# Layer 2's attention: squares and norms of the first head group, times of turnings and outputs, and two longer pauses

## The chip, the cores and the metric

The kernel runs on one core of one Trainium2 chip. The metric is the device time of that core in microseconds. Three runs of the kernel before gave 3033.62, 3033.73 and 3040.51; their median is 3033.73. The profile is of one further execution, with its own time.

## The reference

The input x has the shape (2, 1024, 128) in float32, so there are 2048 tokens of 128 features. The program is a stack of four layers. Each of them adds to x half of a feed-forward block, then an attention (or another mixer of tokens), then half of the same feed-forward block again. The change touches the attention of layer 2, and the norms that open this attention and the second feed-forward block of that layer. Cut to what is computed there:

```python
x = x + 0.5 * _L2_ffn_ref(_layernorm(x), ...)      # 8 experts, 2 per token
x = x + _L2_attn_ref(_layernorm(x), norm_w, Wq, Wkv, Wo, q_gamma, k_gamma)
x = x + 0.5 * _L2_ffn_ref(_layernorm(x), ...)

def _L2_attn_ref(tokens, norm_w, Wq, Wkv, Wo, q_gamma, k_gamma):
    x = tokens * rsqrt(mean(tokens**2, -1) + eps) * norm_w
    q = x @ Wq;  k, v = split(x @ Wkv)              # 16 heads of 64
    q = q / max(norm(q), 1e-12) * (q_gamma + 1) * 8  # norm of each head
    k = k / max(norm(k), 1e-12) * (k_gamma + 1) * 8
    sim = tanh(q @ k.T / 50) * 50 * 64**-0.5         # no mask
    return (softmax(sim) @ v) @ Wo

def _L2_ffn_ref(x, ...):      # per token: the two best of 8 experts
    h = gelu(x @ w1[e] + b1[e]);  res = x + h @ w2[e] + b2[e]
    y = sum over e of gate_e * (layernorm(res) * gamma[e] + beta[e])
```

## The kernel before

**Tokens.** There are two sequences (b = 0, 1) of 1024 tokens, 16 tiles of 128 tokens in all, eight tiles for each sequence. Four tiles form a chunk; the chunks are q = 0 to 3, of which 0 and 1 belong to b = 0. The residual x stays in SBUF all the time.

**Who orders what.** The order of the instructions on TensorE (PE) is written out by hand: the region is under a manual schedule for that engine. The orders of VectorE (DVE), ScalarE (ACT), GpSimd (POOL) and of the DMA issues on SyncE (SP) are chosen by the framework's planner. Each engine then carries out its own instructions in that order and waits wherever an operand or a buffer is not ready.

**Threads.** Work beside the main loop is given as a list of pieces, each a function that issues instructions or a number, which is a pause in planned microseconds. `later` enters such a list as a thread. `tick(us)` moves the planned time forward and lets the first threads in the list issue the pieces whose time has come. `need(key)` issues all that is left of a thread at once.

**Norms.** `norm_pieces` (L183) gives the pieces of one chunk's norm: the statistics (`norm_stats`, with `inv_sqrt` at its end and the offset `ln_off` at L152), a pause `wait[0]`, the application, which writes xn (L162 and L164, L162 on VectorE and L164 on ScalarE), a pause `wait[1]`, four transposes into a PSUM bank pt (L172) and the copy xT. `wait` is (4.5, 4.0) by default, and everywhere in the kernel before. `l2_attn_prep` (L1567) uses it for the attention of one chunk q, `l2_ffn_prep` (L1241) for one of the two chunks (a = 0, 1) of a half of layer 2's feed-forward block; the half's name begins with 1 in the first such block of the layer and with 2 in the second. The second block takes the chunks 0 and 2 as one half and 1 and 3 as the other. `inv_sqrt` (L107) computes a reciprocal square root by Newton's method, in two plus nine small VectorE instructions.

**One group of heads.** `L2Attention.project(b, f)` (L1580) sets up four heads (f = 0 to 3) of one sequence. It returns eight products and eight turnings, one for each tile j. `product(j)` multiplies the normed tokens with the weights for v (pv, L1597) and for q and k (pqk, L1601), copies v (L1598) and q and k (raw, L1608) to SBUF with VectorE, squares raw (sq, L1610) on GpSimd, and sums the squares by head with VectorE into hsq (L1611). The last of the eight also issues the max with 1e-24 (L1614) and `inv_sqrt`, which gives hrq for all eight tiles. `turn(j)` multiplies raw by hrq (L1619, VectorE), transposes q and k with TensorE (four transposes into a bank ppt, L1623) and writes the result, times gamma, to tr (L1626, VectorE).

**The first group.** Its pieces (`first(a)`, a = 0, 1) run as threads inside the last experts of layer 2's first feed-forward block, before the attention's own loop begins. first(0) holds the products 0 to 3; first(1) holds the products 4 to 7 and then all eight turnings.

**The loop.** `run` (L1648) goes through the eight groups, which I count as n = 0 to 7 (b first, then f), each in 16 steps. A step takes two of the group's four heads (p), one half of the queries and two tiles of keys. It issues

- the scores ps (L1687) with a tanh (L1694) on ScalarE for each of two tiles of keys, and one exp (L1695) over both;
- the mix of the step before (po, L1720, TensorE) with the sums of the exponentials: acp on GpSimd (L1707 to L1710), acc on VectorE (L1712 to L1716);
- in every fourth step the division of a finished block: its sums by head in a bank pn (L1732), a copy to rn on ScalarE (L1734), its reciprocal (L1735) and the product aoT (L1736), both on VectorE;
- the pieces that belong to this step: in the steps 0 to 7 one product of the next group each; its eight turnings in the steps 10, 11, 12, 12, 13, 13, 14, 14; and the four pieces of the output of the group before (py, L1664, TensorE) in the steps 8, 8, 9, 9. The second and the fourth of these add a full bank py to four tiles of x (L1673, VectorE);
- `tick(5.8)`.

The last group (n = 7) has no next group; in its step 10 it issues the first two pieces of its own output too. When a group with f = 3 has added its part to x, `done` enters the norms of the second feed-forward block for those chunks. So there are norms in n = 1 (chunks 2 and 3, for the attention of sequence 1) and in n = 4 (the chunks 0 and 1, which group 3's output has finished, for the second feed-forward block).

**PSUM.** There are two buffers for the pairs ps, two for the sums po, and two banks that pt, pv, pqk, ppt, py and pn share in turn.

**Experts and transfers.** An expert step of layer 2 has products ph (L1454), gelu (L1463, ScalarE), products py (L1470) and a result res (L1488), which is stored by SyncE (yd, L1502). `l2_back` (L1524) brings the results back to the tokens with 16 gathers on GpSimd's queue (yg, L1539), which wait for the last such store, and adds them to x with VectorE (L1556).

Of the kernel before, what the change touches and what calls it, by code (L numbers as in the profile page):

```python
# [11 lines left out]
F32 = mybir.dt.float32  # L12
I32 = mybir.dt.int32
BF16 = mybir.dt.bfloat16
AF = mybir.ActivationFunctionType
ALU = mybir.AluOpType
# [5 lines left out]
TB = 8  # L22
# [81 lines left out]
        nc.scalar.copy(out, in_)  # L104


def inv_sqrt(c, out, in_, scale, eps):  # L107


    v = c.nc.vector  # L110
    shape = list(in_.shape)
    flat = int(np.prod(shape[1:]))
    t = c.act.tile(shape, F32, tag=f"nw{flat}", name="nw", bufs=2)
    h = c.act.tile(shape, F32, tag=f"nh{flat}", name="nh", bufs=2)
    v.tensor_scalar(h, in_, scale, eps, ALU.mult, ALU.add)
    v.tensor_scalar(out.bitcast(I32), h.bitcast(I32), -0.5, float(0x5F3759DF), ALU.mult, ALU.add)
    for _ in range(3):
        v.tensor_mul(t, out, out)
        v.scalar_tensor_tensor(t, h, -0.5, t, ALU.mult, ALU.mult)
        v.scalar_tensor_tensor(out, t, 1.5, out, ALU.add, ALU.mult)  # L120
# [1120 lines left out]
def l2_ffn_prep(c, w, keep, h, a):  # L1241
    nc = c.nc
    q, r = h["qs"][a], {}
    tiles = slice(4 * a, 4 * a + 4)
    norm = norm_pieces(c, r, q, by=8)

    def begin():
        if "o" not in h:
            h["o"] = keep.tile([P, 2, TB, 8], F32, tag="ho", name="ho", bufs=2)
            h["g"] = keep.tile([P, 2, TB], F32, tag="hg", name="hg", bufs=2)  # L1250

    def store():
        nc.sync.dma_start(out=h["xd"][512 * a : 512 * a + 512, :].rearrange("(j p) d -> p j d", p=P), in_=r["xn"])

    def chosen():
        h["ready"] += 1
        if h["ready"] == 2:
            c.later(("route", h["name"]), l2_route(c, w, keep, h) + h["then"])

    gates = gate_pieces(  # L1260
        c, r, q, w["router"], 8, w["beta"],
        places=lambda: ([h["o"][:, k, tiles, :] for k in range(2)], [h["g"][:, k, tiles] for k in range(2)]),
    )
    return [begin] + norm[:3] + [store] + norm[3:] + gates[:1] + [chosen] + gates[1:]
# [302 lines left out]
def l2_attn_prep(c, w, rs, q):  # L1567

    e = float(np.finfo(np.float32).eps)
    return norm_pieces(c, rs[q], q, 1.0 + e, 1e-5 * e, w["norm"])  # L1570


class L2Attention:
# [6 lines left out]
    def project(self, b, f):  # L1580


        c, nc, w, rs = self.c, self.c.nc, self.w, self.rs
        side, bank = self.side, c.bank
        mine = self.pool if f % 2 else side
        raw = side.tile([P, TB, 2, 4, 64], F32, tag="raw", name="raw")
        tr = mine.tile([P, 2, 2, S], F32, tag="tr", name="tr", bufs=1)
        v = mine.tile([P, TB, 4, 64], F32, tag="v", name="v", bufs=1)
        ssq = side.tile([P, TB, 2, 4], F32, tag="hsq", name="hsq", bufs=2)
        rq = side.tile([P, TB, 2, 4], F32, tag="hrq", name="hrq", bufs=2)  # L1590

        def product(j):
            c.need((self.key, 2 * b + j // 4))
            lhsT = rs[2 * b + j // 4]["xT"][:, j % 4 * P : (j % 4 + 1) * P]
            pv = bank("pv")[:, 0:256]
            off = 1024 + f * 256
            nc.tensor.matmul(pv, lhsT=lhsT, rhs=w["wkv"][:, off : off + 256], start=True, stop=True)  # L1597
            nc.vector.tensor_copy(v[:, j].rearrange("p h d -> p (h d)"), pv)  # L1598
            pp = bank("pqk").rearrange("p (n h d) -> p n h d", n=2, h=4)
            for n, wt in enumerate((w["wq"], w["wkv"])):  # L1600
                nc.tensor.matmul(  # L1601
                    pp[:, n].rearrange("p h d -> p (h d)"),
                    lhsT=lhsT,
                    rhs=wt[:, f * 256 : (f + 1) * 256],
                    start=True,
                    stop=True,
                )
            nc.vector.tensor_copy(raw[:, j], pp)  # L1608
            sq = side.tile([P, 2, 4, 64], F32, tag="sq", name="sq", bufs=1)
            nc.gpsimd.tensor_mul(sq, raw[:, j], raw[:, j])  # L1610
            nc.vector.tensor_reduce(ssq[:, j], sq, AX.X, ALU.add)  # L1611
            if j == TB - 1:

                nc.vector.tensor_scalar(ssq, ssq, 1e-24, None, ALU.max)  # L1614
                inv_sqrt(c, rq, ssq, 1.0, 0.0)

        def turn(j):
            rj = raw[:, j]
# [16 lines left out]
    def first(self, a):  # L1635

        if a == 0:
            self.ready, self.products, self.turns = self.project(0, 0)
        pieces = []
        for p in self.products[4 * a : 4 * a + 4]:  # L1640
            pieces += [p, 1.0]
        if a == 1:
            pieces.append(3.0)
            for p in self.turns:
                pieces += [p, 1.0]
        return pieces

    def run(self, done, room, even):  # L1648

        c, nc, w = self.c, self.c.nc, self.w  # L1650
        with c.pool("l2a", 2) as pool:
# [94 lines left out]
            for n, (b, f) in enumerate(groups):  # L1746
                (tr, v), aoT = ready, [pool.tile([P, S], F32, tag="aoT", name="aoT", bufs=3) for _ in range(2)]
                slots = [[] for _ in range(16)]
                if n + 1 < len(groups):
                    ready, first, second = self.project(*groups[n + 1])  # L1750
                    for s, piece in enumerate(first):
                        slots[s].append(piece)
                    for s, piece in zip((10, 11, 12, 12, 13, 13, 14, 14), second):
                        slots[s].append(piece)
                for s, piece in zip((8, 8, 9, 9), outs):
                    slots[s].append(piece)
                for s in range(16):
                    k2, often = s % 4, n + 1 == len(groups) and s >= 10
# [504 lines left out]
```

## Time and profile before

| Profiled execution | |
|---|---|
| its own time | 3029.26 us |
| span of its instructions | 3027.5 us |
| mean granted TensorE clock | 0.94 |
| PE busy | 2630.6 us (87%) |
| DVE busy | 2062.3 us (68%) |
| ACT busy | 1596.4 us (53%) |
| POOL busy | 1012.2 us (33%) |
| tanh of layer 2's attention (L1694), 256 of them | 249.0 us, mean 1021 ns |
| exp (L1695), 128 of them | 244.6 us, mean 1911 ns |
| squares (L1610), 64 of them | 88.7 us on POOL, mean 1386 ns |

How to read it: times are microseconds from the start of the span unless they are called ns. A row of the trace gives the start of an instruction, or of several of a kind in a run (x8), the time from its start to its end, the engine, the source line, and what is written and read by the program's names. Brackets at its end hold the time for which the engine stood idle before it, and what it waited for. The granted clock is the share of TensorE's full clock that the chip gave in that stretch. Busy shares are means over stages with different limits; what bounds one stage is read from that stage.

### The profile page before, as it was taken

To read this page: it belongs to the slowest core of one execution; us is meant where nothing else is said; L and a number is where in the kernel's file an instruction comes from. 1 tells how busy PE (TensorE), PEld (TensorE's weight loads), DVE (VectorE), ACT (ScalarE), POOL (GpSimd) and SP (SyncE) were. 2 spreads that over 40 slices of the span, in tenths; PEclk is the share of its full clock that TensorE was granted. 3 is DMA by queue.
4 is the path that set the end of the run, shared out by engine and by line. 5 is a ranking of instruction groups with operands and counts; after the bars stand their busy time and mean duration, and the time that the engine had idled before them with its cause. 6 is when DMAs were issued, how large, how long until landed. Compare 5 with 4: busy or idle time off the path is not lost. (4 is left out here: it accounts for less than half of the span.)

```text
span 3027.5 us, 42431 instructions
## 1 busy us (share of the span) xinstructions
PE 2630.6 (87%) x14226; PEld 1508.3 (50%) x14226; DVE 2062.3 (68%) x6460; ACT 1596.4 (53%) x3188; POOL 1012.2 (33%) x941
## 2 busy tenths in 40 slices
PE   8899999899998888988867569899989996859999
PEld 5544444444574644444447543333434433756667
DVE  5566667666648887688574368867787765557884
ACT  3455555455442465666423327577767784434553
POOL 0133332233104554454333444344434433322110
PEclk9899999999999788999988889899999998979999
DMA  4000000000000000000105510000000012630000
GB/s 122 14 9 14 15 15 15 7 15 15 22 1 0 1 1 1 1 1 1 57 17 153 153 43 1 1 1 1 1 8 1 1 62 74 170 94 21 1 5 11
DMA packets 69768, 86.52 MB, mean 29 GB/s; under 512 B 14334, under 2 KB 49935, under 8 KB 68912
## 3 DMA queue, kind: packets, MB, share of 16 engines
q1 hardware_dynamic: 60816, 71.71, 8.4%
q0 software_dynamic: 4992, 10.27, 1.7%
q8 instruction: 114, 1.87, 0.3%
q10 hardware_dynamic: 3744, 1.84, 0.2%
q14 instruction: 102, 0.84, 0.1%
HBM read 66.18 MB, written 12.38 MB: 26 GB/s over the span
## 5 line engine op out<-in xcount | busy, mean ns | idle before, releaser
L1694 ACT ACTIVATE pe<-ps 128x1024 f32<-128x1024 f32 x256 | 249.0, 1021 | 208.1 <-PE ps L1687 203.3
L518 ACT ACTIVATE pe<-ps,nm 128x512 f32<-128x512 f32 (+3 forms) x384 | 219.8, 578 | 144.9 <-DVE nm L516 121.8
L1687 PE MATMUL ps<-tr 64*128 64x512 f32 x1024 | 263.5, 634 | 0.0
L1720 PE MATMUL po<-pe,v 128*64 128x512 f32 x1024 | 250.1, 609 | 1.4 <-ACT pe L1695 1.4
L1695 ACT ACTIVATE pe<-pe 128x2048 f32<-128x2048 f32 x128 | 244.6, 1911 | 4.0
L348 DVE SCALAR_TENSOR_TENSOR x<-py,gates,x 128x128 f32<-128x128 f32 x448 | 133.3, 344 | 138.7 <-PE py L311 122.7
L516 DVE TENSOR_REDUCE nm<-ps 128x2 f32<-128x256 f32 (+1 forms) x192 | 183.2, 954 | 59.6 <-PE ps L505 55.6
L1454 PE MATMUL ph<-xgT,w1b 128*128 128x128 f32 x736 | 117.4, 311 | 94.0 <-ACT hT L1463 81.4
L505 PE MATMUL ps<-kT,qT 64*128 64x512 f32 (+3 forms) x768 | 180.2, 547 | 16.4 <-ACT pe L518 9.2
L1463 ACT ACTIVATE hT<-ph,w1b 128x128 f32<-128x128 f32 x368 | 105.1, 369 | 160.0 <-issue 112.6
L533 PE MATMUL ptp<-ident,pe 128*128 128x128 f32 x1152 | 172.6, 284 | 16.0 <-ACT pT L104 9.4
L533 PEld LDWEIGHTS ptp<-ident,pe 128*128 128x128 f32 x1152 | 123.8, 141 | 116.6 <-issue 56.2
L547 PE MATMUL po<-pT,v 128*64 128x512 f32 (+3 forms) x768 | 166.7, 513 | 0.0
L1454 PEld LDWEIGHTS ph<-xgT,w1b 128*128 128x128 f32 x736 | 104.4, 219 | 103.5 <-ACT hT L1463 87.0
L1707 POOL TENSOR_TENSOR acp<-pe 128x1024 f32<-128x1024 f32 x32 | 78.3, 2446 | 220.0 <-ACT pe L1695 197.0
L1720 PEld LDWEIGHTS po<-pe,v 128*64 128x64 f32 x1024 | 62.7, 137 | 174.8 <-issue 159.9
L104 ACT COPY pT<-ptp 128x512 f32<-128x512 f32 x192 | 91.9, 478 | 108.2 <-PE ptp L533 107.5
L1396 POOL DMA_INDIRECT xg<-xd,r_tok x92 | 87.6, 952 | 168.2 <-DVE res L1488 96.3
L1687 PEld LDWEIGHTS ps<-tr 64*128 64x128 f32 x1024 | 90.8, 191 | 104.5 <-issue 73.8
L1072 POOL TENSOR_SCALAR pe<-pe,rs 128x256 f32<-128x256 f32 (+7 forms) x128 | 95.2, 757 | 139.4 <-DVE rs L1069 56.0
L311 PEld LDWEIGHTS py<-l3f_w,hT 128*128 128x128 f32 x1024 | 125.6, 195 | 28.1 <-issue 23.3
L1610 POOL TENSOR_TENSOR sq<-raw 128x512 f32<-128x512 f32 x64 | 88.7, 1386 | 147.4 <-DVE raw L1608 113.2
(418 smaller groups left out, 6279.4 us busy)
## 6 DMA issues: line engine op xcount, KB each, us to landing
w1b<-sets SPq DMA_DIRECT2D x92, 258.0 KB
b2g<-sets SPq DMA_DIRECT2D x92, 128.0 KB
two<-two SPq DMA_DIRECT2D x64, 128.0 KB
yd<-y SPq DMA_DIRECT2D x20, 258.0 KB
l2f_w<-in_l2f_w SPq DMA_DIRECT2D x2, 2048.0 KB
sets<-in_l2f_w SPq DMA_DIRECT2D x1, 2048.0 KB
xd<-xn SPq DMA_DIRECT2D x8, 256.0 KB
l3f_w<-in_l3f_w SPq DMA_DIRECT2D x2, 1024.0 KB
```

The source lines that it names most:

```text
L311: nc.tensor.matmul(py[:, j, :], lhsT=hT[:, k, j * P : (j + 1) * P], rhs=w2[:, e, k, :], start=(k == 0), stop=(k == hc - 1),)
L348: c.nc.vector.scalar_tensor_tensor(x, py[:, j, :], rs[q]["g"][:, j, e : e + 1], x, ALU.mult, ALU.add)
L505: nc.tensor.matmul(ps[:, h, :W], lhsT=u["qT"][r, q0 : q0 + P], rhs=u["kT"][r, gk * 512 : gk * 512 + W], start=True, stop=True,)
L516: nc.vector.tensor_reduce(nm, ps[:, :, :W], AX.X, ALU.max, negate=True)
L518: nc.scalar.activation(u["pe", n][:, h, i, :W], ps[:, h, :W], AF.Exp, bias=nm[:, h : h + 1], accum_out=u["rs"][:, n, i, h : h + 1],)
L533: nc.tensor.transpose(pt[:, i * P : (i + 1) * P], u["pe", n][:, h, i, j * P : (j + 1) * P], c.ident)
L547: nc.tensor.matmul(u["po", n][r, lo * P :], lhsT=u["v"][:, BLOCKS[n][1] * 4 + j, cols], rhs=u["pT", n, j][h][:, lo * P :], start=(j == 0), ...
L1454: nc.tensor.matmul(ph[:, a * P : (a + 1) * P], lhsT=t[:, a * P : (a + 1) * P], rhs=xT[n][:, j * P : (j + 1) * P], start=True, stop=True,)
L1687: nc.tensor.matmul(ps[:, h, :], lhsT=tr[r, 1, p, k * P : (k + 1) * P], rhs=tr[r, 0, p, q * 512 : (q + 1) * 512], start=True, stop=True,)
L1694: nc.scalar.activation(pe[:, j], ps, AF.Tanh, scale=1.0 / 50.0)
L1695: nc.scalar.activation(pe, pe, AF.Exp, scale=50.0 * 0.125)
L1720: nc.tensor.matmul(u["po"][r, :], lhsT=u["v"][:, k, 2 * u["p"] + h, :], rhs=pe[:, j, h, :], start=(k == 0), stop=(k == TB - 1),)
```

## The change

It has four parts.

1. *The first group's squares and norms.* For b = f = 0 the squares are computed on ScalarE by an activation with Square in place of GpSimd's product. The max and `inv_sqrt` are issued after the product 3 for the tiles 0 to 3, and after the product 7 for the tiles 4 to 7. `inv_sqrt` gets a `shape`, so that its small tiles for a half keep the size that the whole has. Each half of the products is followed by its own four turnings, so first(0) now holds four products and four turnings, and first(1) the same.
2. *Turnings.* In every group the eight turnings of the next go into the steps 11, 11, 12, 12, 13, 13, 14, 14.
3. *Outputs.* The four pieces go into the steps 8, 8, 10, 10.
4. *Pauses.* `wait` is (9.0, 14.0) in the attention's norms of the chunks 2 and 3, and in the norm of the first chunk (a = 0) of each half of layer 2's second feed-forward block, that is for the chunks 0 and 1.

```diff
-def inv_sqrt(c, out, in_, scale, eps):
+def inv_sqrt(c, out, in_, scale, eps, shape=None):
...
-    shape = list(in_.shape)
+    shape = list(shape or in_.shape)
...
-    t = c.act.tile(shape, F32, tag=f"nw{flat}", name="nw", bufs=2)
-    h = c.act.tile(shape, F32, tag=f"nh{flat}", name="nh", bufs=2)
+    t = c.act.tile(shape, F32, tag=f"nw{flat}", name="nw", bufs=2)[:, 0 : in_.shape[1]]
+    h = c.act.tile(shape, F32, tag=f"nh{flat}", name="nh", bufs=2)[:, 0 : in_.shape[1]]
...
@@ l2_ffn_prep
-    norm = norm_pieces(c, r, q, by=8)
+    norm = norm_pieces(c, r, q, by=8, wait=(9.0, 14.0) if h["name"][0] == "2" and a == 0 else (4.5, 4.0))
...
@@ l2_attn_prep
-    return norm_pieces(c, rs[q], q, 1.0 + e, 1e-5 * e, w["norm"])
+    wait = (4.5, 4.0) if q < 2 else (9.0, 14.0)
+    return norm_pieces(c, rs[q], q, 1.0 + e, 1e-5 * e, w["norm"], wait=wait)
...
@@ L2Attention.project, product(j)
-            nc.gpsimd.tensor_mul(sq, raw[:, j], raw[:, j])
+            if b + f:
+                nc.gpsimd.tensor_mul(sq, raw[:, j], raw[:, j])
+            else:
+                nc.scalar.activation(sq, raw[:, j], AF.Square)
             nc.vector.tensor_reduce(ssq[:, j], sq, AX.X, ALU.add)
-            if j == TB - 1:
-                nc.vector.tensor_scalar(ssq, ssq, 1e-24, None, ALU.max)
-                inv_sqrt(c, rq, ssq, 1.0, 0.0)
+            if j == TB - 1 or b + f == 0 and j == 3:
+                js = slice(0 if b + f else j - 3, j + 1)
+                nc.vector.tensor_scalar(ssq[:, js], ssq[:, js], 1e-24, None, ALU.max)
+                inv_sqrt(c, rq[:, js], ssq[:, js], 1.0, 0.0, ssq.shape)
...
@@ L2Attention.first
-        if a == 1:
-            pieces.append(3.0)
-            for p in self.turns:
-                pieces += [p, 1.0]
+        pieces.append(3.0)
+        for p in self.turns[4 * a : 4 * a + 4]:
+            pieces += [p, 1.0]
...
@@ L2Attention.run
-                    for s, piece in zip((10, 11, 12, 12, 13, 13, 14, 14), second):
+                    for s, piece in zip((11, 11, 12, 12, 13, 13, 14, 14), second):
...
-                for s, piece in zip((8, 8, 9, 9), outs):
+                for s, piece in zip((8, 8, 10, 10), outs):
```

## The prediction

> **What bounds the kernel now.** I began with the page's slices (each digit is the busy tenths of 1/40 of the span, 75.7 us). Layer 2's attention fills slices 25 to 34 of 40, about 1802 to 2545 us:
>
> ```profile
> PE   8899999899998888988867569899989996859999
> ...
> PEclk9899999999999788999988889899999998979999
> ```
>
> TensorE (PE) is at nine tenths in most of them. The page's own chain of waits covers only the last tenth of the span (its shares add up to 10%), so it says nothing here; I went to busy time by stretch (columns: us, then busy time of PE, weight loads, VectorE, ScalarE, GpSimd, then the granted clock):
>
> ```profile
> 1890.00:1980.00 90.00, 78.19 (x326) 32.67 (x324) 70.48 (x160) 55.46 (x49) 31.07 (x17) 0.91 0.00 1
> 1980.00:2070.00 90.00, 87.02 (x394) 35.91 (x392) 67.75 (x79) 64.61 (x54) 42.18 (x21) 1.00 0.00 1
> 2160.00:2250.00 90.00, 80.00 (x362) 34.58 (x360) 70.07 (x125) 58.59 (x54) 37.86 (x19) 0.96 0.01 4
> ```
>
> An undisturbed group of heads (the middle row) is bound by TensorE and has 3 us of 90 to give; the first output products of two such groups start at 2043.11 and 2131.12, so a group takes 88.0. The others lose 10 to 12 us: there a norm or an expert's result lands among the group. I call the groups n = 0 to 7; n = 2, 3, 5 and 6 are undisturbed, n = 1 and 4 are not. Then I read TensorE and VectorE in order of time. Steps 9 to 11 of n = 2 on TensorE (the brackets hold the idle time before the row and what ended it):
>
> ```profile
> 2050.81 2.05 PE L1664 MATMUL py<-l2a_wo,aoT 128*128 128x128 f32 x16 [1.01 <-DVE x L1673]
> ...
> 2056.58 0.66 PE L1623 MATMUL ppt<-ident,raw 128*128 128x128 f32 x4
> ...
> 2062.23 0.66 PE L1623 MATMUL ppt<-ident,raw 128*128 128x128 f32 x4 [1.21 <-DVE x L1673]
> ```
>
> and VectorE in the same steps:
>
> ```profile
> 2050.67 7.69 DVE L1619 TENSOR_TENSOR raw<-raw,hrq 128x512 f32<-128x512 f32 x6
> 2058.29 3.34 DVE L1735 RECIPROCAL rn<-rn 128x512 f32<-128x512 f32 x1
> 2061.55 0.62 DVE L1673 TENSOR_TENSOR x<-x,py 128x512 f32<-128x512 f32 x1
> 2062.09 0.67 DVE L1736 TENSOR_TENSOR aoT<-po,rn 128x512 f32<-128x512 f32 x1
> ...
> 2063.29 1.21 DVE L1712 TENSOR_TENSOR acc<-pe 128x1024 f32<-128x1024 f32 x1
> ```
>
> What to see: both waits of TensorE are for a PSUM bank (there are two) that VectorE's addition of py to x (L1673) has to empty, and the second addition stands directly behind the reciprocal, with aoT and acc behind it. At the start of the attention, TensorE waits, and one square on GpSimd stands in what it waits for:
>
> ```profile
> 1782.21 0.59 PE L1601 MATMUL pqk<-l2a_wkv,xT 128*128 128x256 f32 x2
> 1793.86 1.97 PE L1623 MATMUL ppt<-ident,raw 128*128 128x128 f32 x8 [11.06 <-DVE raw L1619]
> ...
> 1802.62 1.99 PE L1687 MATMUL ps<-tr 64*128 64x512 f32 x8
> ```
>
> ```profile
> 1788.09 1.05 POOL L1610 TENSOR_TENSOR sq<-raw 128x512 f32<-128x512 f32 x1
> ```
>
> That square's input was ready at 1785.74 (the copy L1608 of 1785.06 takes 0.68), but two gathers stood before it on GpSimd. From the last projection to the first scores it takes 20.4 us. Last, the norms in n = 1 and n = 4:
>
> ```profile
> 1956.49 1.11 PE L172 MATMUL pt<-ident,xn 128*128 128x128 f32 x4 [5.12 <-ACT xn L164]
> 2241.58 1.25 PE L172 MATMUL pt<-ident,xn 128*128 128x128 f32 x4 [8.16 <-ACT xn L164]
> ```
>
> ```profile
> 2241.03 1.26 ACT L164 ACTIVATE xn<-x,ln_off,ln_rs 128x128 f32<-128x128 f32 x3 [8.94 <-DVE ln_off L152]
> ```
>
> ScalarE takes its instructions in order: while it waits for ln_off, the tanh and exp behind it wait too, and TensorE behind those.
>
> **The change part by part.** I follow the order in which the changed program is built, engine by engine.
>
> *First group, first half in the experts (a loss).* Its rsqrt and its four turnings now stand before the last experts' products. The reduction of the fourth product ended at 1763.84; then come the max and 11 small instructions of 32 elements. Rows of that width in the trace (L210, L211) take 0.19 and follow each other at 0.225: 12 x 0.225 = 2.7. With one scaling (0.68) the first transpose can start at 1767.2, and the expert's ph behind it on TensorE stood at 1764.75: 2.5 late. Four groups of transposes at 0.57 add 2.3, and a clock drop after this 3.4 us gap about 1.2. Sum: 6.0. The last yd store, the 16 gathers that wait for it and products 4 to 7 move by as much.
>
> *First group, second half (a gain).* After: last projection 0.59, raw copy 0.68, square on ScalarE 0.63 (the square L828 takes 0.685 at 576 elements), reduction 0.69, 12 small ones 2.7, four scalings 2.54, then tr, transpose, tr, transpose on two banks, 1.9: 9.7 instead of 20.4, a gain of 10.7. Products 4 to 7 took 10.1 us and lose the GpSimd waits in between (1.3). So 6.0 - 10.7 - 1.3 = -6.0. GpSimd's 16 gathers at 1.255 then end near 1807 (1803.4 before), and the first square of group 1 is queued behind them; the reduction that waits for it holds VectorE's copies of the next products. With the scores 6 us earlier this costs about 0.5. **I take -5.5, with -9 and 0 as ends.**
>
> [...] The row: the page's profile has loads of 1283 ns (L300, L1911). [...] No row of before shows a square beside a gelu; but the changed program holds as many table loads as before (24), in the same order, so I take no load.
>
> *Turnings from step 11, output at 8 and 10 (a loss).* The wait of 1.01 goes, because py's second half comes a step later. But ppt at step 11 is now two turnings, and the second needs the bank that the second addition to x empties. In the changed program VectorE's order is: six scalings, reciprocal, aoT, acc<-pe, x, acc+acp. For n = 2: TensorE does the same work in steps 8 to 11 without either wait and stands before that turning at 2062.23 - 1.01 - 1.21 = 2060.0. VectorE's scalings do not come earlier (they hang on the norm of the group's heads, before step 9), so the reciprocal ends at 2061.55, aoT 0.60 later, acc 1.15 later, x 0.68 later: 2064.0. **The turning starts 1.8 us later than before, after an idle stretch of 4.0 us.** Nothing later takes it back: before, no wait over 0.3 follows in the group.
>
> Idle stretches cost clock. The rows (last stretch, PEclk third from the end):
>
> ```profile
> 2056.00:2064.00 8.00, 6.79 (x34) 1.00 0.00 0
> 1872.40:1876.00 3.60, 3.55 (x12) 0.55 0.01 2
> ```
>
> The gap of 1.21 left the clock full; that of 2.41 (before 1872.45) gave 0.55 for 3.6 us, and 2.59 (before 2264.26) 0.64 for 4.0. A gap of 4.0 then costs 3.6 x 0.45 = 1.6. [...] I take the row. **+13.6; ends -8.9 (both waits simply go, 4 x 2.22) and +16.**
>
> *n = 0 (nothing).* It has no output. The wait of 2.40 before its first turning goes, but the turnings at step 12 wait for tr behind the same VectorE chain: its reciprocal ends at 1867.9, then aoT, acc, acc+acp, tr: 1871.8, and TensorE is there at 1867. Step 12 ends near 1873 as before. 0, ends -2.4 and +1.8.
>
> *Longer pauses, n = 1.* The two transposes pt go three steps later. xn keeps its place on ScalarE, so ScalarE still waits for ln_off (7.0 and 5.3 us). TensorE gains 1.19 + 1.12 at the first, and at the second goes on with one step of scores until it meets the held tanh; the stall at step 11 takes some back. Between 0 and -8; I take -3.
>
> *Longer pauses, n = 4.* Here xn moves behind exp. Waits of 8.16, 0.88, 2.59 and 0.35 (12.0) stand against a wait of 6.4 at step 11 (the same chain with the norm's small instructions in it: x ends near 2242.8, TensorE is there at 2236.4) and gate work now among the next group's products. Between 0 and -12; I take -5.
>
> *End.* py's second half meets the last group's own output: +0.5, within 1 either way.
>
> Sum: -5.5 + 13.6 + 0 - 3 - 5 + 0.5 = +0.6. Against the profiled execution (3029.26, of which the span is 3027.5) that is 3029.9; the runs' median is 3033.73, the sum on it **3034**.
>
> **The rivals.**
> 1. *Slower.* The step-11 stall also decides n = 1 and n = 4, and the pauses give nothing: 6 x 3.4 - 5.5 + 0.5 = +15.4, 3049. For it: VectorE is busiest there (70 of 90). Against: the waits for xn are larger than the stall. It decides once x lands in these groups later than ScalarE's wait for ln_off ended before.
> 2. *Faster: the moved steps do what they say.* The four groups lose 2.22 each: 3034 - 13.6 - 8.9 = 3012. For it: nothing waits at py any more. Against: VectorE's built order.
> 3. *Faster: the pauses remove all of TensorE's waits for xn:* 6.3 and 12.0 instead of 3 and 5, 3034 - 10.3 = 3024. Against: ScalarE still stands before ln_off.
> 4. *The start gives nothing,* GpSimd's gathers being the head of the first steps: 3034 + 5.5 = 3039.5.
>
> **How the numbers follow.** A measurement of this kernel tells about 0.3% (9 us) from no change. Likeliest case 0.42 (its own range 3027 to 3041), rival 4 0.13: both within 0.3%, 0.55. Rivals 2 (0.13) and 3 (0.12): faster 0.25. Rival 1: slower 0.20. The range reaches down between rivals 2 and 3 to 3016 and up to rival 1's 3049; outside lie most of rival 2 and the upper half of rival 1.
>
> **What would show it.** First scores near 1797 with the last gather near 1807; squares of about 0.63 on ScalarE with no table load beside them; at step 11 of n = 2, 3, 5, 6 a wait of about 4 us for x with the clock near 0.5 after it, and groups 91.4 apart instead of 88.0; ScalarE still idle before xn in n = 1. I am wrong if groups come out at 86 (rival 2), or if first scores come at 1802 or later.

## The result: 3045.91 us, 0.4% slower

The changed kernel takes 3045.91 us (median of five runs, 3044.02 to 3052.21). The kernel before takes 3035.61 in the same comparison (3033.62 to 3040.51). The ratio is 1.0039 with a 95% interval of 1.0027 to 1.0051: a loss of 10.3 us in the medians, small and real. The prediction's likeliest case was 3034, with a range of 3016 to 3049; the time lies inside the range, but on the side to which I gave 0.2.

The profiled execution of the changed kernel took 3044.02 with a span of 3042.1. Read first, as before, was the busy time by stretch (columns as in the prediction). The first row is the stretch of 90 us that was undisturbed before; the others go in pieces of 4 us through step 11 of group n = 2:

```profile
1980.00:2070.00 90.00, 85.31 (x374) 35.23 (x374) 66.65 (x77) 61.43 (x51) 39.38 (x20) 0.96 0.00 1
2054.00:2058.00 4.00, 0.28 (x3) 0.05 (x1) 3.97 (x4) 0.97 (x1) 0.00 (x0) 0.92 0.00 0
2058.00:2062.00 4.00, 3.50 (x10) 1.91 (x12) 3.97 (x6) 0.27 (x1) 0.00 (x0) 0.50 0.00 0
2062.00:2066.00 4.00, 4.00 (x16) 1.02 (x13) 1.17 (x1) 3.35 (x3) 0.00 (x0) 0.73 0.00 0
```

TensorE was busy for 87.02 of that stretch and is now busy for 85.31; its clock fell from 1.00 to 0.96. In the second row it does next to nothing (0.28 of 4.00), and in the two rows after that it works at a clock of 0.50 and 0.73. TensorE in order of time shows the same place (n = 2, steps 10 to 12; lines are seven to eight higher in this kernel, so L1671 is py, L1631 ppt and L1694 ps):

```profile
2047.86 2.05 PE L1671 MATMUL py<-l2a_wo,aoT 128*128 128x128 f32 x16
...
2053.63 0.66 PE L1631 MATMUL ppt<-ident,raw 128*128 128x128 f32 x4
2058.50 1.12 PE L1631 MATMUL ppt<-ident,raw 128*128 128x128 f32 x4 [4.22 <-DVE x L1680]
2059.55 3.79 PE L1694 MATMUL ps<-tr 64*128 64x512 f32 x8
```

The wait of 1.01 at py is gone. In place of it and of the 1.21 in step 11, the second turning of step 11 waits 4.22 for the addition to x, and the scores behind it take 3.79 where they take 1.99 at full clock. VectorE in the same steps:

```profile
2045.02 7.71 DVE L1627 TENSOR_TENSOR raw<-raw,hrq 128x512 f32<-128x512 f32 x6
2052.65 3.34 DVE L1742 RECIPROCAL rn<-rn 128x512 f32<-128x512 f32 x1
2056.03 0.69 DVE L1743 TENSOR_TENSOR aoT<-po,rn 128x512 f32<-128x512 f32 x1
2056.63 1.22 DVE L1719 TENSOR_TENSOR acc<-pe 128x1024 f32<-128x1024 f32 x1
2057.77 0.68 DVE L1680 TENSOR_TENSOR x<-x,py 128x512 f32<-128x512 f32 x1
```

This is the order that the prediction read from the built program: scalings, reciprocal, aoT, acc, and only then x (L1680), which empties the bank. The start of the attention, on TensorE and ScalarE:

```profile
1766.34 0.63 PE L1631 MATMUL ppt<-ident,raw 128*128 128x128 f32 x4 [3.29 <-DVE raw L1627]
...
1792.16 1.97 PE L1631 MATMUL ppt<-ident,raw 128*128 128x128 f32 x8 [5.97 <-DVE raw L1627]
...
1796.51 2.67 PE L1694 MATMUL ps<-tr 64*128 64x512 f32 x8
```

```profile
1787.13 0.63 ACT L1617 ACTIVATE sq<-raw 128x512 f32<-128x512 f32 x1 [1.41 <-DVE raw L1611]
```

The first scores start at 1796.51 in place of 1802.62, and a square takes 0.63 on ScalarE.

Last, the norms in n = 1 and n = 4 on ScalarE:

```profile
1953.35 0.88 ACT L165 ACTIVATE xn<-x,ln_off,ln_rs 128x128 f32<-128x128 f32 x2 [8.42 <-DVE ln_off L153]
```

```profile
2243.85 1.26 ACT L165 ACTIVATE xn<-x,ln_off,ln_rs 128x128 f32<-128x128 f32 x3 [9.71 <-DVE ln_off L153]
```

ScalarE stands before xn no shorter than it did (8.42 here and 5.29 before for the second norm of n = 1, 9.71 and 8.94 for the first of n = 4); TensorE waits for xn at the transposes pt in neither group any more; where it waits now is told under "The pauses".

Where the time went is read from the starts of the scores. I counted from the first product of the first group (so that what lies ahead of the attention drops out), and measured each group from its step 4 to the next group's step 4, which makes one period of a group whole:

| Stretch | before | after | difference |
|---|---|---|---|
| first product to first scores | 58.50 | 51.68 | -6.8 |
| first scores to step 4 of n = 0 | 20.7 | 23.0 | +2.3 |
| n = 0 | 88.51 | 89.26 | +0.8 |
| n = 1 | 104.98 | 102.37 | -2.6 |
| n = 2 | 88.01 | 92.63 | +4.6 |
| n = 3 | 88.17 | 92.38 | +4.2 |
| n = 4 | 108.11 | 106.99 | -1.1 |
| n = 5 | 88.00 | 91.59 | +3.6 |
| n = 6 | 81.53 | 85.10 | +3.6 |
| step 4 of n = 7 to the last scores | 57.7 | 59.3 | +1.6 |
| first product to last scores | 784.29 | 794.35 | +10.1 |

The attention alone accounts for +10.1, as much as the medians differ. The two profiled executions differ by 14.8 (3044.02 and 3029.26); the rest lies outside the attention, where the program is the same. There, runs of one kernel differ by several microseconds too: the profiled execution of before was 4.4 faster than the fastest of the five runs in this comparison.

### The profile page after: what moved, and what is told of

Same layout as the page of the kernel before. It is cut to its first block, busy times and chain, and to the rows that moved or that the text cites. A ratio compares the mean times of both kernels' runs of the same rounds, so it can differ in the third digit from the quotient of the medians.

```text
span 3042.1 us, 42448 instructions
## 1 busy us (share of the span) xinstructions
PE 2630.8 (86%) x14226; PEld 1511.2 (50%) x14226; DVE 2061.9 (68%) x6472; ACT 1601.2 (53%) x3196; POOL 1001.5 (33%) x933
## 5 line engine op out<-in xcount | busy, mean ns | idle before, releaser
L1694 PE MATMUL ps<-tr 64*128 64x512 f32 x1024 | 270.9, 649 | 0.8 <-issue 0.5
L517 DVE TENSOR_REDUCE nm<-ps 128x2 f32<-128x256 f32 (+1 forms) x192 | 183.2, 954 | 59.3 <-PE ps L506 55.3
L1465 ACT ACTIVATE hT<-ph,w1b 128x128 f32<-128x128 f32 x368 | 105.0, 369 | 149.8 <-issue 95.5
L1694 PEld LDWEIGHTS ps<-tr 64*128 64x128 f32 x1024 | 92.9, 196 | 114.1 <-issue 79.3
L312 PE MATMUL py<-l3f_w,hT 128*128 128x128 f32 x1024 | 129.3, 280 | 7.3 <-issue 4.9
```

The lines of the kernel that those rows point to most:

```text
L312: nc.tensor.matmul(py[:, j, :], lhsT=hT[:, k, j * P : (j + 1) * P], rhs=w2[:, e, k, :], start=(k == 0), stop=(k == hc - 1),)
L517: nc.vector.tensor_reduce(nm, ps[:, :, :W], AX.X, ALU.max, negate=True)
L1694: nc.tensor.matmul(ps[:, h, :], lhsT=tr[r, 1, p, k * P : (k + 1) * P], rhs=tr[r, 0, p, q * 512 : (q + 1) * 512], start=True, stop=True,)
```

## The experiments

All verdicts are against the kernel before on the same chip. Kernels that are set against the same time of the kernel before shared a chip. On one chip, where the kernel before took 2944.21, the experts' stages ran faster, so its times are only compared with each other. The groups of the attention took the same time on all chips: with turnings, outputs and VectorE's work as before, groups 2 and 5 are 88.0 everywhere. Where a number is given for a group, it is from step 4 to step 4 as in the table, in one profiled execution of that kernel.

### Which of the two moves costs the time

Turnings alone:

```diff
-  zip((10, 11, 12, 12, 13, 13, 14, 14), second)
+  zip((11, 11, 12, 12, 13, 13, 14, 14), second)
```

> The kernel before with only the turnings moved (steps 11, 11, 12, ...). Theory (the loss is the pair of moves: with both, VectorE's second addition of py to x stands behind reciprocal, aoT and acc, and the second turning of step 11 waits for it): alone, this move leaves that addition directly behind the reciprocal; the waits of about 1.0 at py and 1.2 at the second turning stay, and groups 2, 3, 5 and 6 keep 88.0 us each; whole kernel within 4 us of before. Rival (each move costs by itself, half of the 16 us that the four groups lost): groups of about 90 us, whole kernel +8. Rival (the move of turnings is the loss): groups of 92, +16.

Measured: 3037.94 against 3033.17, ratio 1.0015 (1.0005 to 1.0025). Groups 2, 3, 5 and 6 take 88.01, 88.16, 88.01 and 81.53: not one of them moved by more than 0.01 against before. The waits stayed too, on TensorE of group 2:

```profile
2058.23 2.05 PE L1664 MATMUL py<-l2a_wo,aoT 128*128 128x128 f32 x16 [1.00 <-DVE x L1673]
...
2069.65 0.66 PE L1623 MATMUL ppt<-ident,raw 128*128 128x128 f32 x4 [1.21 <-DVE x L1673]
```

Moving the turnings costs and gains nothing by itself in these groups. The whole kernel is 4.8 slower, a little more than the 4 that the theory allowed. The attention took 787.5 from the first product, 3.2 more than before, of which 2.4 lie ahead of step 4 of group 0, where the edit changes nothing; I come back to that. What the rest of the 4.8 is, no run here shows.

Outputs alone:

```diff
-  zip((8, 8, 9, 9), outs)
+  zip((8, 8, 10, 10), outs)
```

> The kernel before with only the output pieces moved (steps 8, 8, 10, 10). Theory: the wait at py goes, the first turning stays in step 10, and the second, in step 11, needs the bank of the first, whose copy tr now stands behind reciprocal and aoT on VectorE: a wait of about 2.8 in place of 1.0 + 1.2, with a clock drop of about 1.4 behind it: groups of 88.0 + 0.6 + 1.4 = 90, four of them +8. Rival (this move alone is the whole loss): groups of 92, +16. Rival (the move only removes the wait): groups of 87, -4.

Measured: 3043.49 against 3033.17, ratio 1.0031 (1.0019 to 1.0044). The groups take 90.45, 91.81, 90.45 and 82.33, that is +2.4, +3.6, +2.4 and +0.8. In group 2 the turning waits 3.27 for the copy tr, and the clock falls behind it:

```profile
2069.11 0.66 PE L1623 MATMUL ppt<-ident,raw 128*128 128x128 f32 x4 [3.27 <-DVE tr L1626]
2069.69 3.39 PE L1687 MATMUL ps<-tr 64*128 64x512 f32 x8
```

So this move alone is a loss, by another operation (tr, L1626) that stands behind the same reciprocal. The four lose 9.3 in all where the theory had 8 and the rivals 16 and -4. These four also show what the clock is worth. The wait is 3.3 to 3.4 in all of them, but in n = 6 the clock stayed at 1.00 behind it, and that group lost only 0.8; behind the others it fell (0.63, 0.50 and 0.57 in the 4 us from the turning on in n = 2, 3 and 5), and they lost 2.4 to 3.6.

Both moves, with nothing else changed:

> The kernel before with both moves, and neither the change to the first group nor the pauses. Theory: the four groups take 88.0 + 4.0 = 92 as in the changed kernel, with a gap of about 4.2 in step 11 and a clock near 0.5 after it; groups 1 and 4 lose up to 3 each, the last about 1.6: +17 to +24 against before. Rival (the stall comes from the new start or the pauses, which shift the work on VectorE): 88 a group, within 4 us of before.

Measured: 3050.5 against 3033.17, ratio 1.006 (1.0043 to 1.0077), 17.3 slower. The groups take 92.90, 92.61, 92.11 and 85.66: +4.9, +4.4, +4.1 and +4.1, 17.6 in all. The stall needs neither the new start nor the pauses. Groups 1 and 4 lost nothing (104.41 and 106.31, against 104.98 and 108.11); there the theory was wrong.

The two moves taken back, start and pauses kept:

> The changed kernel with turnings and outputs put back (steps 10, 11, 12, ... and 8, 8, 9, 9). Theory: first scores 6 to 7 us earlier, 2 to 3 of it given back in the first four steps of group 0; group 1 gains 3 to 6 from the pauses; group 4 gains 10 and gives some 9 back in the first steps of group 5; four groups at 88.0. Sum -4.5 - 4 - 1.5 = -10 against before, faster by about 0.3%. Rival (the loss sits in the start or in the pauses): not faster than before.

Measured: 3026.88 against 3033.17, ratio 0.998 (0.9967 to 0.9993), 6 faster. The four groups are back at 88.01, 88.01, 88.01 and 81.52. The loss of the change is these two moves together; the rest of it is a gain. It is smaller than the 10 that were expected: the attention came 4.5 faster, since group 0 gave back 4.4 of the earlier start and not 2 to 3, and group 4 gained nothing (108.75).

### What stands in the way in step 11

First the reciprocal is taken out of the chain:

```diff
-  nc.vector.reciprocal(rn, rn)
+  nc.vector.tensor_scalar(rn, rn, 0.0, 1.0 / 1024, ALU.mult, ALU.add)
```

> The changed kernel with the reciprocal of the softmax sums (3.34 us on VectorE) replaced by a cheap operation that writes the constant 1/1024. This leaves out the division by the sums, so what follows the attention sees other values and only the groups of the attention are read. Theory (the second turning of step 11 waits for the chain reciprocal, aoT, acc, x on VectorE): the gap of 4.2 in groups 2, 3, 5 and 6 shrinks by about 2.9 to 1.3, TensorE's clock stays full after it, and these groups take 92.3 - 2.9 - 2.6 = 86.8 from step 4 to step 4. Rival (the gap belongs to something else, such as the bank's own turn or ScalarE): groups of 92 and a gap of 4 as before.

VectorE and TensorE of this kernel, group 2:

```profile
2011.35 0.41 DVE L1742 TENSOR_SCALAR rn<-rn 128x512 f32<-128x512 f32 x1
2011.80 0.69 DVE L1743 TENSOR_TENSOR aoT<-po,rn 128x512 f32<-128x512 f32 x1
2012.40 1.22 DVE L1719 TENSOR_TENSOR acc<-pe 128x1024 f32<-128x1024 f32 x1
2013.54 0.68 DVE L1680 TENSOR_TENSOR x<-x,py 128x512 f32<-128x512 f32 x1
```

```profile
2014.27 0.66 PE L1631 MATMUL ppt<-ident,raw 128*128 128x128 f32 x4 [1.29 <-DVE x L1680]
```

This is one execution of a kernel that leaves the division out, read for its groups alone. The operation takes 0.41 in place of 3.34, and the wait shrinks by the same 2.93, from 4.22 to 1.29. Behind a gap of 1.29 the clock stays at 1.00. Groups 2, 3 and 5 take 87.0, where 86.8 was expected. The wait is for VectorE's chain, and for no bank's own turn.

The second cause was the length of the scalings ahead of the reciprocal: 7.71 for six, where the first two took 1.29 (0.645 each). Here GpSimd's additions acp are left out in the block of steps 8 to 11, and with them VectorE's addition of acp to acc (1.22):

```diff
+  late = u["p"] == 1 and u["q"] == 0
-  if k2 == 0:
+  if k2 < 2 and late:
+      pass
+  elif k2 == 0:
...
-  nc.vector.tensor_add(acc, acc, acp)
+  if not late:
+      nc.vector.tensor_add(acc, acc, acp)
```

> The changed kernel without GpSimd's three additions acp in the block of steps 8 to 11, which leaves out the first half of that block's softmax sums; only the groups are read. Theory (VectorE's chain is late because its two-operand instructions hold while GpSimd adds: six scalings took 7.7 and not 6 x 0.645 = 3.9, one Newton step 2.25 and not 0.23): the scalings fall to 0.65 each, the reciprocal of step 9 begins about 5.9 earlier, the gap of 4.2 in step 11 and the clock drop vanish, groups 2, 3, 5 and 6 take about 85.5. Rival (the scalings are long for another reason): scalings of 1.28, groups of 92.

```profile
2031.33 0.22 DVE L120 SCALAR_TENSOR_TENSOR nw<-nh,nw 128x64 f32<-128x64 f32 x1
...
2035.21 3.69 DVE L1627 TENSOR_TENSOR raw<-raw,hrq 128x512 f32<-128x512 f32 x6
```

In this one execution six scalings take 3.69 and the Newton step 0.22. In the changed kernel that step took 2.25, beside the first of GpSimd's additions:

```profile
2038.87 2.40 POOL L1714 TENSOR_TENSOR acp<-pe 128x1024 f32<-128x1024 f32 x1 [1.47 <-ACT pe L1702]
```

```profile
2039.10 2.25 DVE L120 SCALAR_TENSOR_TENSOR nw<-nh,nw 128x64 f32<-128x64 f32 x1
```

Without the additions the groups take 85.51, 85.51, 85.51 and 79.03, as expected, and in group 2 TensorE waits nowhere in steps 8 to 12. These are the times of a group without any stall, and they allow a second sum: 92.63 - 85.51 = 7.1, of which 4.22 is the wait and 2.9 the clock (0.65 over the 8.00 us behind the wait, which is 2.8).

Like the Newton step, the scalings are held beside an addition. In the changed kernel GpSimd's other two additions

```profile
2044.63 2.36 POOL L1716 TENSOR_TENSOR acp<-acp,pe 128x1024 f32<-128x1024 f32 x1 [3.36 <-ACT pe L1702]
2047.07 2.70 POOL L1717 TENSOR_TENSOR acp<-acp,pe 128x1024 f32<-128x1024 f32 x1
```

run from 2044.63 to 2049.77, over the first two of the six scalings. These take 2.53 and 2.86, where the median of the eight is 0.68, and each ends some 0.55 after the addition beside it. Not every operation of VectorE is held: the reciprocal at 1979.90 in the changed kernel took 3.34 with two such additions beside it, as it does without them, and the copy tr at 1983.16, beside the second of them, took 0.63. What decides between the two kinds, no run here shows.

### The start

Norm and turnings of the first group in halves, but with the squares left on GpSimd; turnings, outputs and pauses as before:

```diff
-  nc.scalar.activation(sq, raw[:, j], AF.Square)
+  nc.gpsimd.tensor_mul(sq, raw[:, j], raw[:, j])
```

> The kernel before with the first group's norms and turnings in halves, but its squares left on GpSimd (turnings, outputs and pauses as before). From the same expert product to the first scores the kernel before takes 72.3 us, the changed one 65.5. Theory (most of the gain is the norm in halves, the squares on ScalarE only save waits behind the gathers): 67.5 to 69.5. Rival (the squares are the gain): 72 or more. Rival (they give nothing): 65.5.

This expectation was set from an expert's product, which on this faster chip stands elsewhere (the same measure gave 82.2 here and 75.5 for the run with ScalarE's squares that shared the chip, so that the squares are worth 6.7 by it). I therefore read it from the first product of the first group to the first scores. Without any change that stretch took 58.5, 58.6, 58.9 and 58.8 (four kernels); with squares on ScalarE it took 51.4 to 52.1 in nine; with halves and squares on GpSimd it took 60.1. One execution took 2948.41, where the kernel before has 2944.21 on that chip. The theory was wrong and the rival that puts the gain in the squares right: against the run that shared the chip (51.4), the squares are worth 8.7, more than the whole gain of 7, and the halves without them lose about 1.4 (there is no trace of the kernel before on that chip; the 58.5 to 58.9 are from the other). From the last projection's end to the first scores it takes 19.8 before, 15.5 with halves alone, and 10.3 with both. The halves do gain at the end, but they spend it earlier, in the experts, where their rsqrt and turnings come ahead of the last products; the squares on ScalarE gain in the projections and behind the gathers.

What the start gained is partly given back in the first steps of group 0: from first scores to step 4 it takes 20.7 to 23.0 in the four kernels with the old start, and 22.0 to 26.1 in the nine with the new one. Not all of that belongs to the start. In the kernel with only the turnings moved, the first mix of group 0 waits 2.07 and then runs for 3.22, where before it waited 1.42 and ran for 1.94, with the same program in both. From the scores ahead of that mix to the pqk behind it takes 8.11 there and 5.81 before, so that such a wait and the slower products behind it account for some 2 us from one kernel's trace to another's.

### The pauses

The feed-forward norm's pauses put back, start and the attention's pauses kept:

> Start and the longer pauses of the attention's norms alone: the changed kernel with turnings, outputs and the feed-forward norm's pauses put back. Theory (the feed-forward pauses only move 10 us of waits from group 4 to the first steps of group 5): from step 4 of group 4 to step 4 of group 5 it takes 108.1 as in the kernel before, against 108.75 with these pauses; whole kernel within 3 us of the run with both pauses, 8 faster than before. Rival (these pauses are worth the forecast 5 once the stall is gone): 5 slower than with both.

Measured: 2934.48 against 2944.21, ratio 0.9966 (0.9952 to 0.9981), 9.7 faster. Group 4 takes 106.44 without these pauses and 108.75 with them. In other kernels that leave its norms and its outputs alone it takes 108.1 to 110.3, so that a gain of 2.3 from taking them away is not settled, but the forecast gain of 5 from having them is not there. Why they give nothing is to be seen in the run with both pauses (TensorE and ScalarE, group 4):

```profile
2236.06 3.68 PE L1727 MATMUL po<-pe,v 128*64 128x512 f32 x8 [8.03 <-ACT pe L1702]
```

```profile
2233.72 0.49 ACT L165 ACTIVATE xn<-x,ln_off,ln_rs 128x128 f32<-128x128 f32 x1 [8.93 <-DVE ln_off L153]
```

The wait of 8.16 at the transposes pt is gone, and TensorE waits 8.03 at the mix po: ScalarE still stands 8.93 before xn until ln_off is there, with the exp that po needs queued behind it. The pauses moved TensorE's place of waiting, not ScalarE's. Two pairs of kernels that differ in the pauses of both norms, and in the start, say the same of the time: group 4 takes 108.75 with them and 108.11 without where turnings and outputs are as before, and 106.99 with and 106.31 without where both are moved.

In the changed kernel, with its other order of VectorE, group 4 did come 10.0 faster from its step 4 to its end, and lost 8.9 of that in the first four steps of group 5. Only part of either number is waiting: TensorE's idle time fell by 5.3 in the first stretch and rose by 3.1 in the second, and much of the rest are products of the gates that moved from the one to the other. In group 5 the gates of the delayed norms lie among the products (ScalarE, then TensorE):

```profile
2283.70 0.21 ACT L245 ACTIVATE t2m<-t2m 128x4 f32<-128x4 f32 x1 [2.49 <-DVE t2m L244]
```

```profile
2287.28 0.70 PE L1604 MATMUL pqk<-l2a_wq,xT 128*128 128x256 f32 x2 [2.94 <-ACT rn L1741]
...
2289.43 3.67 PE L1694 MATMUL ps<-tr 64*128 64x512 f32 x8
```

A tanh stands behind a gate's exp (which waits 2.49 for t2m), the sums' copy rn behind that tanh and an exp, TensorE waits 2.94 for rn, and the scores after it take 3.67 in place of 1.99.

For the attention's own norms the pauses gain: group 1 takes 101.8 to 103.0 in four kernels that have them (the changed one, the one with both pauses, the one with the attention's alone, and the one with group 4's outputs moved), and 104.4 to 105.0 in the five that don't. Where VectorE's own work or the other outputs were changed as well, it lies between 97.6 and 105.7, so the gain of some 2.6 is shown for those four only. ScalarE's waits are not what went: they are 7.04 and 8.42 in the changed kernel and were 7.04 and 5.29. Of TensorE's, the 1.19 at the first pt is gone, but the 5.12 at the second has become one of 4.12 at the sums pn, for the addition to x:

```profile
1954.93 1.97 PE L1739 MATMUL pn<-acc,ones 128*64 128x512 f32 x4 [4.12 <-DVE x L1680]
1956.84 2.72 PE L1694 MATMUL ps<-tr 64*128 64x512 f32 x8
```

Added up over the group, TensorE is idle for 11.1 in place of 12.1; the other 1.6 of the gain is the same work done in less time, as in the scores behind this wait, which take 2.72 where those behind the wait of 5.12 took 3.79.

### Versions that follow from this

Outputs away from the reciprocal, turnings later:

```diff
-  zip((10, 11, 12, 12, 13, 13, 14, 14), second)
+  zip((11, 12, 12, 13, 13, 14, 14, 15), second)
-  zip((8, 8, 9, 9), outs)
+  zip((3, 3, 6, 6), outs)
```

> The same as the run with start and the attention's pauses alone, but with output pieces in the steps 3, 3, 6, 6, away from the reciprocal of step 9, and turnings in the steps 11, 12, 12, 13, 13, 14, 14, 15. Theory (a turning costs nothing while no bank that it needs hangs on an operation queued behind the reciprocal): the waits of 1.0 and 1.2 go, groups 2, 3, 5 and 6 take 85.8, whole kernel 9 faster than without it and 17 faster than before. Rival (VectorE's work between the norm and the last tr is the limit): the wait moves to steps 12 to 14, groups stay at 88, 8 faster than before.

Measured: 2958.66 against 2944.21, ratio 1.0048 (1.0033 to 1.0064), slower. The groups take 92.39, 92.19, 93.07 and 86.46. The waits at py and in step 11 are gone, and one of 5.01 for tr stands in step 12. Outputs in the steps 3 and 6 put 2 us each ahead of the last products, and with them the norm and all that follows from it came later. The rival was right about the place, and both were wrong about the size.

All outputs in step 8:

```diff
-  zip((10, 11, 12, 12, 13, 13, 14, 14), second)
+  zip((10, 11, 12, 13, 13, 14, 14, 15), second)
-  zip((8, 8, 9, 9), outs)
+  zip((8, 8, 8, 8), outs)
```

> Start and the attention's pauses alone, with all four output pieces in step 8 and turnings in the steps 10, 11, 12, 13, 13, 14, 14, 15. Theory (both additions to x then stand ahead of the reciprocal, and the norm is not delayed as it was with outputs in the steps 3 and 6): no wait for x in the steps 9 to 11, groups of 86 to 87.5, 10 to 17 faster than before. Rival (the copies tr behind reciprocal and acc hold the turnings of steps 12 and 13): groups of 88 to 90.

Measured: 3040.81 against 3034.84, ratio 1.0029 (1.0014 to 1.0043), slower. The groups take 88.08, 88.08, 88.07 and 82.84. Both additions to x do stand ahead of the reciprocal, but now the sums pn wait 2.12 for acc, which stands behind tr and takes 3.07 in one addition beside GpSimd's first addition of the next block, in place of 1.22. Group 4 takes 112.88. The rival was right about the number, but the turnings were not what waited.

Outputs later in group 4 alone:

```diff
-  zip((8, 8, 9, 9), outs)
+  zip((8, 8, 10, 10) if n == 4 else (8, 8, 9, 9), outs)
```

> Start and the attention's pauses alone, with output pieces in the steps 8, 8, 10, 10 in group 4 only. Theory (in group 4, where the norm's chain on VectorE holds TensorE anyway, the later output costs nothing and its move was worth 3.05 with outputs moved alone): group 4 takes 103 to 105 in place of 106.4 to 108.1, whole kernel 11 faster than before. Rival (that gain hung on the stalls of the other groups): 106 to 108, 8 faster than before.

Measured: 3025.16 against 3034.84, ratio 0.9959 (0.994 to 0.9977), 9.7 faster. Group 4 takes 105.08, on the theory's edge, and the whole is as fast as without this edit on another chip (0.9966). It is no more than a hint, since the two were not run on one chip.

GpSimd's three additions of steps 8 to 11 given to VectorE, with start and the attention's pauses, and everything else as before:

```diff
+  eng = nc.vector if u["p"] == 1 and u["q"] == 0 else nc.gpsimd
-  nc.gpsimd.tensor_add(acp, pe[:, 0], pe[:, 1])
+  eng.tensor_add(acp, pe[:, 0], pe[:, 1])
...
-  nc.gpsimd.tensor_add(acp, acp, pe[:, 0])
-  nc.gpsimd.tensor_add(acp, acp, pe[:, 1])
+  eng.tensor_add(acp, acp, pe[:, 0])
+  eng.tensor_add(acp, acp, pe[:, 1])
```

> Start and the attention's pauses alone (turnings, outputs and feed-forward pauses as before), with the same three additions acp moved from GpSimd to VectorE. Theory (an addition costs VectorE 1.22 if it does it, and about 2 if GpSimd does it beside two-operand work): reciprocal about 3 earlier, the waits of 1.0 and 1.2 go, groups of about 86 in place of 88.0; with the gains of start and pauses, 17 faster than before. Rival (VectorE has no room for 3 x 1.22 more): groups of 88 or more, 8 faster than before or less.

```profile
2043.98 1.22 DVE L1716 TENSOR_TENSOR acp<-pe 128x1024 f32<-128x1024 f32 x1
2045.12 0.68 DVE L1680 TENSOR_TENSOR x<-x,py 128x512 f32<-128x512 f32 x1
2045.71 4.30 DVE L1627 TENSOR_TENSOR raw<-raw,hrq 128x512 f32<-128x512 f32 x7
2049.93 1.22 DVE L1718 TENSOR_TENSOR acp<-acp,pe 128x1024 f32<-128x1024 f32 x1
2051.07 3.35 DVE L1744 RECIPROCAL rn<-rn 128x512 f32<-128x512 f32 x1
```

Measured: 3012.21 against 3034.84, ratio 0.9913 (0.9892 to 0.9934), 22.6 faster than before, where 17 was expected, and so faster than both kernels. VectorE does three additions more, 1.22 each, two of them ahead of the reciprocal, and still comes to the reciprocal earlier: 9.8 us after the first Newton step (2041.30 to 2051.07), where the kernel before takes 13.5 (2044.76 to 2058.29) and the changed one 13.6 (2039.10 to 2052.65). Seven scalings take 4.30, where six took 7.7. The groups take 85.65, 85.66, 85.65 and 79.18, 0.14 above those without any stall. The theory was right, and the gain larger. In the four groups it is some 2.35 each, 9.4 in all: with the same start and pauses and the additions on GpSimd they take 88.01, 88.01, 88.01 and 81.53.

## Why the prediction was right and wrong

The time lies inside the range, but in part by luck. The likeliest case, 3034, was 12 too low, and the upper end that takes 3045.91 in was that of rival 1, whose reason, a loss in n = 1 and n = 4, did not come. By its own steps, with the differences of the table above:

| Step of the prediction | forecast | measured |
|---|---|---|
| first group, to step 4 | -5.5 | -4.5 (-6.8, then +2.3) |
| turnings and outputs, n = 2, 3, 5, 6 | +13.6 | +16.0 |
| n = 0 | 0 | +0.8 |
| pauses, n = 1 | -3 | -2.6 |
| pauses, n = 4 | -5 | -1.1 |
| end | +0.5 | +1.6 |
| sum | +0.6 | +10.1 |

**The mechanism of the large step was right.** The place, the operation that is late (x behind reciprocal, aoT and acc), the length of the gap (4.0 forecast, 4.20 to 4.22 in all four groups) and its dependence on both moves came out as read from VectorE's order and were confirmed by taking each of them alone, both together, and the reciprocal away. Its size was off in one term: the clock after the gap was put at 1.6, the value of the shorter gaps of before. Against the 85.51 (79.03 in n = 6) of groups without a stall, less the gap, it was 2.9, 2.7, 1.9 and 1.9 in n = 2, 3, 5 and 6: the clock fell behind each of the four gaps, to 0.50, 0.50, 0.55 and 0.63 over 3.6 us. The 13.6 is 4 x (1.8 + 1.6), for the later turning and for the clock, and the row behind the 1.6 was a choice. It rests on the gaps of 2.41 and 2.59, and the trace of before has one of 2.40 (before 1860.51) with a full clock behind it:

```profile
1860.50:1864.00 3.50, 3.49 (x18) 1.00 0.02 5
```

In n = 0 two waits of 2.40 and 2.41 became one of 5.50 at step 12, and the group took 0.8 more where nothing was forecast.

**The step that failed is "Longer pauses, n = 4".** It let xn's move behind exp remove part of the 12.0 us of waits, and took -5 between 0 and -12. ScalarE's own wait for ln_off was left where it was, and TensorE met it at the mix (8.03 in the run with both pauses); in the changed kernel what group 4 gained was lost again in group 5, whose products then shared their steps with the gates. The lower end, 0, was the right one, though the gates had been named as a reason against the gain. Even the measured -1.1 is not the pauses': the two moves without any pause took group 4 from 108.11 to 106.31, and start and pauses put 0.7 on that. The wait of 6.4 in step 11 that this step forecast beside them came as 6.69.

The start was nearly right as a sum, and by its parts: 9.7 forecast and 10.9 measured from the start of the last projection to the first scores (10.3 from its end), 6.0 and 5.0 lost by the halves between products 3 and 4, 1.3 and 1.3 gained in products 4 to 7. Another 1.0 was gained in products 0 to 3, which the sum had at nothing. The 1.2 for the clock among the 6.0 was an estimate of mine, and no row of before shows it; in the changed kernel the gap there was 3.29, and the clock was 0.75 over the 6.96 us behind it, which is 1.7. Table loads did not appear: the profile has as many before as after (24), four of the squares stand among gelus (1746.62 to 1761.19) with no load between, and a square took 0.63. But the cost of the backlog afterwards, 0.5 forecast, is 2.3 in this pair of traces; it can't be told well from the fall of the clock in the same steps (0.73 in the first 2.59 us).

**The rivals.** None came true as written. Rival 1's time (3049) is the nearest, and half of its mechanism holds, since the pauses of n = 4 gave nothing; but n = 1 and n = 4 did not lose: their sums fell, though TensorE's wait for x in step 11 of n = 4 is the longest of that group (6.69). Rival 2 fails with the groups at 92, rival 3 with ScalarE's wait for ln_off, and rival 4 with the start's 4.5. The likeliest case had a sum 9.5 too low, and all six terms erred to the same side: 3.9 of it is n = 4, 2.4 the gap and the clock, 1.1 the end, 1.0 the start, 0.8 n = 0 and 0.4 n = 1.

## What to carry to other kernels

A piece moved to a later step must be followed to the operation that frees its buffer, in the built order of the engine that does it: here two waits of 2.2 in all became one of 4.2, because the freeing addition, which stood behind the reciprocal, went behind aoT and acc as well. One of the moves alone cost these groups nothing and the other 9.3, where both cost 17.6. When a pause moves an instruction that waits, with others queued behind it on its engine, ask whether that engine's wait goes, or only the place where others meet it: ScalarE stood 8.94 before xn without the pauses and 8.93 with them. And where two engines seem to share work, time the shared stretch: taking three additions off GpSimd let VectorE, which got them, reach its reciprocal 3.8 us sooner.

## What the runs showed that I had not expected

GpSimd's additions hold VectorE in the kernel before as well, and that sets the period of a group there: with turnings and outputs as before and the three additions on VectorE, a group takes 85.65 in place of 88.0. In that kernel, too, a Newton step of 64 elements that takes 0.23 took 2.25 beside one of them. I had seen long scalings in the trace of before and costed them as they stood.

TensorE's clock fell behind all eight gaps of 4.2 to 4.4 us (four in the changed kernel, to between 0.50 and 0.63; four in the one with both moves alone, where the scores behind them take 3.71 to 3.79 in place of 1.99), at a price of 1.9 to 2.9 us in the changed kernel. Behind shorter gaps it fell or did not: it did behind 2.07 (a mix of 3.22 in place of 1.94), 2.41 (0.55) and 3.27 (0.63), and did not behind 2.40 in the kernel before and 3.28 in n = 6 of the one with the outputs moved (1.00 in both). Behind 1.29 and 1.42 it stayed full (1.00). So gaps of like length did not cost the same time, and no length of gap is found here at which the clock begins to fall.

The experts' stages ran at another speed on one chip: one and the same kernel before took 3033 to 3036 on three comparisons and 2944 on a fourth, while groups 2 and 5 of the attention took 88.0 on all chips wherever their outputs and VectorE's work were as before. In two kernels that differ by the feed-forward pauses alone, the experts' first products ph waited 81.0 in all on the one chip and 22.5 on the other. Why the chips differ, no run here shows.
